# Cross-attention on one core: head groups of 3 and 2, keys stored once, and earlier refills

## The chip, the cores and the metric

The kernel runs on one core of a Trainium2 chip. The core has a matrix engine (PE), a vector engine (DVE), an activation engine (ACT), GpSimd (POOL) and a queue engine (SP) that issues most of the DMAs. Each engine works through its own list of instructions in order and waits for the others by semaphores. The metric is the time of one execution on the device in microseconds (us); lower is better.

## The reference, cut to what matters

Four attentions are computed in the original layer (text, object, others, IP), but the context given here has 77 tokens and the text part takes the first 77. The other three get no keys, so their sums are empty and add nothing. What remains is one cross-attention with a projection, a bias and a residual:

```python
q = heads(x @ to_q_w)              # x: 32 x 512 x 640, 20 heads of 32
k = heads(ctx @ to_k_w)            # ctx: 32 x 77 x 1024
v = heads(ctx @ to_v_w)
p = softmax(q @ k.T / sqrt(32))    # per head, 512 queries x 77 keys
out = merge(p @ v) @ to_out_w + to_out_b + x
```

All arrays are float32.

## The kernel before

Each float32 operand of a matmul is split into a high and a low part (`split`), and a product is made of three matmuls: high by high, high by low, low by high (`PAIRS`).

**The fill.** The context has 32 x 77 = 2464 tokens, cut into five groups of up to 512 columns (`GROUPS_KV`, the last is number `LAST`). For each, keys and values are projected for the five chunks j of 128 columns (four heads each). `split_keys` splits a chunk of keys in a tile `ks` (two buffers) and writes it to DRAM (`k_dram`), by five DMAs; those of the earlier groups are issued by POOL, those of the last by SP. `split_values` does the same for `v_dram`. The values of the last group are left over: their chunks are made by `context_values(LAST, j, psv)`, one before the first slot and four within slots 0, 1 and 2 (`beside`).

**The slots.** Then come 160 slots n, one for each batch b (0 to 31) and chunk j (0 to 4), written out by hand in `slot`. A slot holds four sets of scores (`scores(n, t)`, L478, 128 queries each): three matmuls of the query tile `qt` against the key tile `kb`, a maximum on DVE (`nm`, L486), four exponentials on ACT (L496). Between the sets PE makes the queries of the next slot (`queries`, L443), the values of slot n - 4 (`values`, L570) and eight of the forty steps of an earlier batch's output projection (`piece`, `project`, L613). DVE transposes the probabilities in blocks (`transpose_p`, L518, tile `z`); four DMAs write them to a DRAM tile `pd` (L525), and two more read them back transposed as `raw` (`load_p`, L534 and L535), two slots later. ACT, DVE and POOL split `raw` into `pp` (L542, L548, L549, L556) at the start of the slot that uses it, before that slot's exponentials.

**Keys and values by groups.** The five chunks are in two groups, j = 0, 1 and j = 2, 3, 4 (`GROUPS`). Each group has one tile of keys (`kb`) and one of values (`vb`), which are refilled in place for the next batch, so a refill must follow the last reader and precede the first. `refill(b, j, part)` says in which slot what is loaded, half of it at the start of the slot (part 0) and half in its middle (part 1): values of group 1 in slot j = 0, keys of group 1 in slot 1, values of group 0 in slot 2, keys of group 0 of the next batch in slot 3. Scores use the keys in the slot of their own j; values are used four slots later.

The key tile has four planes: two hold the high parts twice, since the first score matmul reads planes 0 and 3 (`kb[:, 0::3]`) and the others read planes 1 and 2, in which high and low parts of the two pairs of heads lie in opposite halves of the partitions. `k_dram` has three planes, laid out so that one DMA a head fills three planes of `kb`.

**The order of the rest.** SP issues nearly everything: the `pd` writes, `raw`, keys, values, the batch's x (`load_x`, in four quarters of the columns, `xs`), the residual rows (`xr`, L602, three buffers) and the results (L648). Tables in the code fix the slot of each: `TRANSPOSE_X` (DVE transposes of x, in three places of a slot), `SPLIT_X`, `RESIDUAL`, `BIAS` (POOL adds the bias to the residual), `PIECES`, `WO` (the output weights, first used in batch 1).

Of the kernel before, what the change touches and what calls it, by code (L numbers as in the profile page):

```python
# [8 lines left out]
F32 = mybir.dt.float32  # L9
FPR = mybir.dt.float32r  # L10
# [13 lines left out]
P = 128  # L24
Q = 32
HEADS = 20
HD = 32
NKEY = 77
HPC = 4
# [14 lines left out]
    (1, 1, 96, 2, 0, 32),  # L44
]

GROUPS = ((0, 2), (2, 3))
GROUP_OF = (0, 0, 1, 1, 1)


@with_exitstack
def kernel(
# [25 lines left out]
    nc = tc.nc  # L78
    B, S, C = x.shape
    CA = ehs.shape[2]  # L80
    NT = B * NKEY
# [12 lines left out]

    k_dram = [dram.tile([P, 3, nj, NT], FPR, name=f"k_dram{j0}") for j0, nj in GROUPS]

    v_dram = dram.tile([NT + KPAD - NKEY, HPC, NC_, 3, HD], FPR, name="v_dram")
    wo_dram = dram.tile([P, NC_, 2, C], FPR, name="wo_dram")  # L100
# [106 lines left out]
    def split_keys(g, j):  # L207
        g0, gn = GROUPS_KV[g]
        ks = kvt.tile([P, 2, G], FPR, tag="ks", name="ks")
        split(ks[:, 0, :gn], ks[:, 1, :gn], pks.pop(j)[:, :gn])  # L210
        engine = nc.gpsimd if g + 1 < len(GROUPS_KV) else nc.sync
        j0 = GROUPS[GROUP_OF[j]][0]
        dst = k_dram[GROUP_OF[j]].rearrange("(h r) s c n -> r s h c n", h=2)[
            :, :, :, j - j0, g0 : g0 + gn
        ]
        engine.dma_start(dst[:, 0].bitcast(F32), ks[:64, :, :gn].bitcast(F32))
        engine.dma_start(dst[:, 1, 0].bitcast(F32), ks[:64, 0, :gn].bitcast(F32))
        engine.dma_start(dst[:, 1, 1].bitcast(F32), ks[64:, 0, :gn].bitcast(F32))
        for half in range(2):
            engine.dma_start(dst[:, 2, half].bitcast(F32), ks[64:, 1 - half, :gn].bitcast(F32))  # L220

    def values_of(g, j, pool):

# [21 lines left out]
    def context_values(g, j, pool):  # L245
        values_of(g, j, pool)
        split_values(g, j)
# [3 lines left out]
    def load_x(b, quarters=range(4)):  # L251

        if b not in xss:
            xss[b] = xpool[0].tile([P, S // Q, C // 4], F32, tag="xs", name="xs")
        xs = xss[b]
        src = x[b].rearrange("(a j) (q u) -> q j a u", j=Q, q=4)
        for q in quarters:
            nc.sync.dma_start(xs[q * Q : (q + 1) * Q, :, :], src[q])
# [158 lines left out]
    def load_keys(b, g, heads=range(HPC)):  # L417
        j0, nj = GROUPS[g]
        src = k_dram[g][:, :, :, b * NKEY : (b + 1) * NKEY].bitcast(F32)
        for i in heads:  # L420
            r, half = slice(i * HD, (i + 1) * HD), i % 2 * NKEY
            nc.sync.dma_start(  # L422
                kbs[g][r, i // 2 : i // 2 + 3, :, half : half + NKEY].bitcast(F32), src[r]
            )

    def load_values(b, g, segments=SEGMENTS):
        j0, nj = GROUPS[g]
# [63 lines left out]
    def exps(n, t, sc, nm):  # L491
        if t == 0:
            sms[n] = main.tile([P, NQ * HPC], F32, tag="sm", name="sm", bufs=2)
        for i in range(HPC):
            at = t * HPC + i
            nc.scalar.activation(  # L496
                pnb[n % 2][:, at, :NKEY],
                sc[:, i * NKEY : (i + 1) * NKEY],
                AF.Exp,
                bias=nm[:, i : i + 1],  # L500
                accum_out=sms[n][:, at : at + 1],
            )
# [102 lines left out]
    def add_bias(b, t):  # L605
        nc.gpsimd.tensor_tensor(xrs[b, t], xrs[b, t], bias, ALU.add)  # L606
# [48 lines left out]


    PIECES = {3: (1, 0), 4: (1, 2), 0: (2, 4), 1: (2, 6), 2: (2, 8)}
    RESIDUAL = {2: (1, 0), 3: (1, 1), 4: (1, 2), 0: (2, 3)}
    BIAS = {3: (1, 0), 4: (1, 1), 0: (2, 2), 1: (2, 3)}
    TRANSPOSE_X = {0: ((), (0,), ()), 1: ((1,), (2,), ()), 2: ((3,), (), ())}  # L660
    SPLIT_X = {2: ((0,), (1,)), 3: ((2, 3), (4,))}

    WO = {4: (0,), 5: (1, 2), 6: (3, 4)}
    wos = []

    def take(m):
# [5 lines left out]
    def refill(b, j, part):  # L672

        heads = range(2 * part, 2 * part + 2)
        segments = SEGMENTS[4 * part : 4 * part + 4]
        if j == 0 and b:
            load_values(b - 1, 1, segments)
        elif j == 1:
            load_keys(b, 1, heads)
        elif j == 2:  # L680
            load_values(b, 0, segments)
        elif j == 3 and b + 1 < B:
            load_keys(b + 1, 0, heads)

    def slot(n, beside=()):
        b, j = divmod(n, NC_)
        ahead, more = n + 1 < N, b + 1 < B
        back, first = PIECES[j]
        bo_, has_out = b - back, b >= back
        xsplits = SPLIT_X.get(j, ((), ())) if more and n > 2 else ((), ())  # L690
        turns = TRANSPOSE_X.get(j, ((), (), ())) if more and b else ((), (), ())
        if b == 1 and j < 2:
            turns = (((), (), ()), ((0, 1), (2,), ()))[j]
        taken = takes.get(n)

        filling = taken is not None and not has_out
        if not filling:
            refill(b, j, 0)
        if taken is not None:
            cast_p(taken)  # L700
        if n - 1 in takes:
            high_a(takes[n - 1])
        bias_now = j in BIAS and b >= BIAS[j][0]
        if bias_now and (j == 3 or not ahead):
            add_bias(b - BIAS[j][0], BIAS[j][1])
        s = scores(n, 0)
        if j == 2:
            finish()
        if taken is not None:
            rest_p(taken)  # L710
        rs = sums(n - 1) if n else None
        if taken is not None:
            last_p(taken)
        if n:
            normalize(n - 1, rs)
        if n - 1 in takes:
            low_a(takes[n - 1])
        exps(n, 0, *s)
        if ahead:
            queries(n + 1, 0, 2)  # L720
        s = scores(n, 1)
        if n >= LATE:
            load_p(n - LAG + 1)
        if filling:
            refill(b, j, 0)
        if n == NC_:
            load_x(b + 1, (2, 3))
        for k in WO.get(n, ()):
            nc.sync.dma_start(wos[0][:, k].bitcast(F32), wo_dram[:, k].bitcast(F32))
        refill(b, j, 1)  # L730
        finish()
        if j == 4 and b and b + 2 < B:
            load_x(b + 2, (0, 1))
        if j in RESIDUAL and b >= RESIDUAL[j][0]:
            load_residual(b - RESIDUAL[j][0], RESIDUAL[j][1])
        exps(n, 1, *s)
        for i in turns[0]:
            transpose_x(b + 1, i)
        if ahead:
            queries(n + 1, 2, NC_)  # L740
        s = scores(n, 2)
        if not ahead:
            exps(n, 2, *s)
            piece(bo_, first)
            finish()
            s = scores(n, 3)
        early = ahead and has_out and j in (1, 4)
        if early:
            piece(bo_, first)
            finish()  # L750
        if not ahead:
            transpose_p(n - 1)
        if ahead:
            split_q(n + 1)
            if bias_now and j != 3:
                add_bias(b - BIAS[j][0], BIAS[j][1])
            exps(n, 2, *s)
        if n and not has_out:
            transpose_p(n - 1)
        if j == 4 and b + 2 < B:  # L760
            load_x(b + 2, (0, 1) if not b else (2, 3))
        for c in xsplits[0]:
            split_x(b + 1, c)
        if not ahead:
            exps(n, 3, *s)
            normalize(n, sums(n))
            finish()
            piece(bo_, first + 1)
            values(taken)
            sum_a(taken)  # L770
            return
        if has_out:
            if not early:
                piece(bo_, first)
        else:
            s = scores(n, 3)
        if taken is not None:
            values(taken)
        if len(beside) > 0:
            context_values(LAST, beside[0], psv)  # L780
        if has_out:
            s = scores(n, 3)
            transpose_p(n - 1)
        finish()
        for i in turns[1]:
            transpose_x(b + 1, i)
        if taken is not None:
            sum_a(taken)
        for c in xsplits[1]:
            split_x(b + 1, c)  # L790
        exps(n, 3, *s)
        if len(beside) > 1:
            context_values(LAST, beside[1], psv)
        if has_out:
            piece(bo_, first + 1)
        for i in turns[2]:
            transpose_x(b + 1, i)
# [86 lines left out]
        close(3)  # L884

    load_keys(0, 0)
    queries(0, 0, NC_)
    split_q(0)
    context_values(LAST, 0, psv)
# [1 line left out]
        transpose_x(1, i)  # L891
    for c in range(2):
        split_x(1, c)
    slot(0, (1,))
    slot(1, (2,))
    slot(2, (3, 4))
    kva.release()
    lw = ctx.enter_context(tc.tile_pool(name="lw", bufs=1, reuse_waits="tile"))
    wos.append(lw.tile([P, NC_, 2, C], FPR, name="wo_s"))
    psv.release()  # L900
    kvp.release()
    late.append(ctx.enter_context(tc.tile_pool(name="late", bufs=1, reuse_waits="tile")))
# [46 lines left out]
```

## Time and profile before

| what | us |
|---|---|
| median of 3 runs | 2124.54 |
| lowest and highest run | 2122.19, 2130.13 |
| profiled execution | 2130.74 |
| its span, first to last instruction | 2129.0 |
| PE busy in it | 1941.3 (91%) |
| weight loads of PE | 1716.1 (81%) |
| DVE busy | 1581.1 (74%) |
| ACT busy | 1552.7 (73%) |
| POOL busy | 1268.1 (60%) |
| first score matmul | 302.8 |

The span is what the profile explains; the profiled execution's own time is 1.7 us longer. The DMA queue that the hardware serves was busy for 79.5% of the span of its 16 engines, and the granted clock of PE was 0.953 of full speed on the mean. Busy shares are means over the fill and the slots, which have different limits, so a stretch has to be looked at by itself.

### The profile page before, as it was taken

What the parts mean: (1) busy time and instruction counts of PE and PEld (TensorE: products, weight loads), DVE (VectorE), ACT (ScalarE), POOL (GpSimd) and SP (SyncE); (2) the same over time, 40 slices, a digit from 0 to 9 for tenths busy, and PEclk for the clock granted to TensorE, in tenths of its full rate; (3) what the DMA queues carried; (4) which work ended last, traced back from release to release, by engine and by line L of the source; (5) the groups of instructions that cost most, each with busy time, mean ns of one, the idle gap of its engine ahead of it and who ended that gap; (6) DMA issues with size and microseconds to landing.
All of it is one profiled execution on the core that took longest, in us unless ns stands there. A gap on an engine that the chain in (4) does not pass through costs nothing.

```text
span 2129.0 us, 37333 instructions
## 1 busy us (share of the span) xinstructions
PE 1941.3 (91%) x10332; PEld 1716.1 (81%) x10332; DVE 1581.1 (74%) x2494; ACT 1552.7 (73%) x6210; POOL 1268.1 (60%) x1068
## 2 busy tenths in 40 slices
PE   9898978799999999999999999999999999999998
PEld 7776867688888888888888888888888888888887
DVE  4344336688788788887888888888878888888784
ACT  3232137788788788888888888888878888888782
POOL 1212246566666666666666666666767766666663
PEclk9999989899999999999999999999999999999999
DMA  9978868888788888888888888888888888888875
GB/s 183 207 188 230 202 142 195 216 215 215 203 214 219 205 218 213 213 216 212 221 223 214 208 220 218 217 218 208 223 207 217 211 216 209 215 216 212 210 202 150
DMA packets 584926, 443.96 MB, mean 209 GB/s; under 512 B 209104, under 2 KB 491792, under 8 KB 584720
## 3 DMA queue, kind: packets, MB, share of 16 engines
q1 hardware_dynamic: 577648, 421.83, 79.5%
q0 software_dynamic: 6976, 19.59, 3.3%
q8 instruction: 85, 1.39, 0.3%
q14 instruction: 121, 0.99, 0.1%
q10 hardware_dynamic: 96, 0.16, 0.0%
HBM read 253.48 MB, written 187.95 MB: 207 GB/s over the span
## 4 chain that ended last, share of the span: by engine, by line
PE 56%; DMA 17%; DVE 8%; SPq 8%; ACT 6%; issue 3%; POOL 1%; DVEq 0%; ACTq 0%; POOLq 0%
PE pq L443 21%; PE po L613 16%; PE sc L478 8%; PE pa L570 6%; DMA kb<-k_dram 5%; PE pk L191 5%; DMA raw<-pd 4%; SPq L422 2%; ACT pn L496 2%; DMA pd<-z 2%; DMA xs<-in_x_dram 2%; DMA k_dram<-ks 2%; DVE z L518 2%; SPq L525 2%; PE pv L191 1%
## 5 line engine op out<-in xcount | busy, mean ns | idle before, releaser
L496 ACT ACTIVATE pn<-sc,nm 128x77 f32<-128x77 f32 x2560 | 801.3, 332 | 123.5 <-DVE nm L486 114.0
L443 PE MATMUL pq<-xt,wq_s 128*128 128x512 f32 x2400 | 665.5, 421 | 0.1
L613 PE MATMUL po<-wo_s,at 128*128 128x320 f32 x3840 | 639.1, 315 | 9.8 <-DVE xr L642 4.0
L613 PEld LDWEIGHTS po<-wo_s,at 128*128 128x128 f32 x3840 | 570.5, 190 | 19.1 <-DVE at L595 10.8
L496 ACT ACTIVATION_READ_ACCUMULATOR pn<-sc,nm 128x1 f32 x2560 | 538.8, 210 | 0.0
L443 PEld LDWEIGHTS pq<-xt,wq_s 128*128 128x128 f32 x2400 | 459.5, 203 | 85.0 <-POOL xt L270 0.5
L478 PEld LDWEIGHTS sc<-kb,qt 128*128 128x128 f32 x1920 | 339.8, 197 | 201.1 <-issue 112.7
L556 POOL TENSOR_TENSOR pp<-raw,pp 64x512 fp32r<-64x512 f32 x160 | 225.1, 1407 | 439.7 <-ACT pp L548 362.9
L478 PE MATMUL sc<-kb,qt 128*128 128x154 f32 (+1 forms) x1920 | 330.8, 282 | 146.4 <-DMA kb<-k_dram 99.0
L486 DVE TENSOR_REDUCE nm<-sc 128x4 f32<-128x308 f32 x640 | 295.1, 466 | 163.1 <-PE sc L478 152.4
L511 POOL TENSOR_TENSOR pn<-pn,rs 128x1232 f32<-128x1232 f32 x160 | 364.4, 2277 | 49.1 <-DVE rs L506 38.5
L460 DVE TENSOR_TENSOR qt<-pq,qt 64x512 fp32r<-64x512 f32 x320 | 220.2, 688 | 110.2 <-ACT qt L454 105.1
L570 PE MATMUL pa<-pp,vb 128*128 128x512 f32 x960 | 253.3, 399 | 5.6 <-DMA vb<-v_dram 4.1
L518 DVE STREAM_TRANSPOSE z<-pn 128x1280 f32<-128x1280 f32 x160 | 241.8, 1512 | 21.0 <-DMA pd<-z 13.9
L270 POOL TENSOR_TENSOR xt<-xs,xt 128x512 fp32r<-128x512 f32 x160 | 203.8, 1292 | 86.3 <-ACT xt L269 60.3
L583 DVE TENSOR_TENSOR pa<-pa,aw 64x512 f32<-64x512 f32 x320 | 222.7, 696 | 28.0 <-ACT aw L581 17.7
L549 DVE TENSOR_TENSOR pp<-raw,pp 128x1024 fp32r<-128x1024 f32 x160 | 212.1, 1325 | 28.5 <-ACT pp L542 28.5
L542 ACT CAST pp<-raw 128x1024 fp32r<-128x1024 f32 x160 | 168.6, 1054 | 84.2 <-DMA raw<-pd 84.1
L458 POOL CAST qt<-qt 64x512 fp32r<-64x512 f32 x320 | 195.4, 610 | 48.7 <-ACT qt L454 30.9
L606 POOL TENSOR_TENSOR xr<-xr,bias 128x640 f32<-128x640 f32 x128 | 200.4, 1567 | 12.9 <-PE sc L478 2.9
L581 ACT COPY aw<-pa 64x1024 f32<-64x1024 f32 x160 | 162.0, 1013 | 59.7 <-PE pa L570 56.2
L570 PEld LDWEIGHTS pa<-pp,vb 128*128 128x128 f32 x960 | 174.6, 189 | 36.8 <-DMA vb<-v_dram 4.6
(47 smaller groups left out, 1550.6 us busy)
## 6 DMA issues: line engine op xcount, KB each, us to landing
pd<-z SPq DMA_DIRECT2D x640, 160.0 KB, 3.3
raw<-pd SPq DMA_DIRECT2D x160, 512.0 KB, 4.4
xs<-in_x_dram SPq DMA_DIRECT2D x128, 320.0 KB, 8.1
xr<-in_x_dram SPq DMA_DIRECT2D x128, 320.0 KB, 3.8
out_dram<-xr SPq DMA_DIRECT2D x127, 320.0 KB, 3.7
raw<-pd SPq DMA_DIRECT2D x160, 128.0 KB, 4.6
v_dram<-vs SPq DMA_DIRECT2D x80, 192.0 KB, 4.0
kb<-k_dram SPq DMA_DIRECT2D x128, 86.6 KB, 4.9
```

Of the source, the lines that this page charges most:

```text
L443: nc.tensor.matmul(pqs[n], wq_s[:, k, a, j * P : (j + 1) * P], xts[b, k][:, c, :], start=(k == 0 and m == 0), stop=(k == NC_ - 1 and m == 2),)
L460: nc.vector.tensor_tensor(qt[r, 1 + w, :], pq[r], qt[r, 0, :].bitcast(F32), ALU.subtract)
L478: nc.tensor.matmul(sc[:, cols], qt[:, m, t * P : (t + 1) * P], keys_, start=(m == 0), stop=(m == 2),)
L486: nc.vector.tensor_reduce(nm, sc[:, :KCOLS].rearrange("p (h k) -> p h k", k=NKEY), AX.X, ALU.max, negate=True)
L496: nc.scalar.activation(pnb[n % 2][:, at, :NKEY], sc[:, i * NKEY : (i + 1) * NKEY], AF.Exp, bias=nm[:, i : i + 1], accum_out=sms[n][:, at : ...
L511: nc.gpsimd.tensor_tensor(pf, pf, rs.unsqueeze(2).to_broadcast([P, NQ * HPC, NKEY]), ALU.mult)
L518: nc.vector.transpose(z.rearrange("p b t j -> p t b j"), pn.rearrange("p (t h) k -> p t (h k)", t=NQ).rearrange("p t (b i) -> p t b i", i=Q),)
L549: nc.vector.tensor_tensor(pp[:, 2:4, :], raw[:, 0:2, :], pp[:, 0:2, :].bitcast(F32), ALU.subtract)
L556: nc.gpsimd.tensor_tensor(pp[64:, 4, :], raw[:64, 2, :], pp[:64, 4, :].bitcast(F32), ALU.subtract)
L570: nc.tensor.matmul(pas[n][:, p, :], vb[:, p, t, :], pp[:, c, :], start=(c == p), stop=(t == 1),)
L583: nc.vector.tensor_tensor(pa[64 * p : 64 * p + 64, 0], pa[:64, p], aw[:, p], ALU.add)
L613: nc.tensor.matmul(pos[b, t, h][:, :HALF], ats[b * NC_ + j][:, a, t * P : (t + 1) * P], wos[0][:, j, c, h * HALF : (h + 1) * HALF], start= ...
```

## The change

Head groups become j = 0, 1, 2 and j = 3, 4. `k_dram` has two planes, high and low, as `ks` has them, and is written by one DMA. A head's keys are loaded by two DMAs, one for each part, into planes 1 and 2 of `kb`; the second copies of the high parts (planes 0 and 3) are made by two GpSimd copies, in slot 1 for group 1 and in slot 4 for group 0.

The refills move: keys of group 1 to slot 0, values of group 1 to slot 1; values of group 0 stay in slot 2 and keys of group 0 in slot 3. The last quarter of x is loaded at the start of slot 0 instead of the end of the slot 4 before it, and the transposes of x move later. The first residual and its bias are handled one slot earlier. The output weights are loaded a chunk a slot from slot 1 on. Two chunks of the last group's values are made before slot 0, and one beside each of the slots 0, 1 and 2; the tile of the output weights is allocated after slot 0.

```diff
-GROUPS = ((0, 2), (2, 3))
-GROUP_OF = (0, 0, 1, 1, 1)
+GROUPS = ((0, 3), (3, 2))
+GROUP_OF = (0, 0, 0, 1, 1)
...
-    k_dram = [dram.tile([P, 3, nj, NT], FPR, name=f"k_dram{j0}") for j0, nj in GROUPS]
+    k_dram = [dram.tile([P, 2, nj, NT], FPR, name=f"k_dram{j0}") for j0, nj in GROUPS]
...
-        dst = k_dram[GROUP_OF[j]].rearrange("(h r) s c n -> r s h c n", h=2)[
-            :, :, :, j - j0, g0 : g0 + gn
-        ]
-        engine.dma_start(dst[:, 0].bitcast(F32), ks[:64, :, :gn].bitcast(F32))
-        engine.dma_start(dst[:, 1, 0].bitcast(F32), ks[:64, 0, :gn].bitcast(F32))
-        engine.dma_start(dst[:, 1, 1].bitcast(F32), ks[64:, 0, :gn].bitcast(F32))
-        for half in range(2):
-            engine.dma_start(dst[:, 2, half].bitcast(F32), ks[64:, 1 - half, :gn].bitcast(F32))
+        engine.dma_start(
+            k_dram[GROUP_OF[j]][:, :, j - j0, g0 : g0 + gn].bitcast(F32), ks[:, :, :gn].bitcast(F32)
+        )
...
         for i in heads:
-            r, half = slice(i * HD, (i + 1) * HD), i % 2 * NKEY
-            nc.sync.dma_start(
-                kbs[g][r, i // 2 : i // 2 + 3, :, half : half + NKEY].bitcast(F32), src[r]
-            )
+            own, half = slice(i * HD, (i + 1) * HD), slice(i % 2 * NKEY, (i % 2 + 1) * NKEY)
+            other = slice(*((i + 2) % HPC * HD + k for k in (0, HD)))
+            for part, rows in enumerate((own, other)):
+                nc.sync.dma_start(kb[rows, 1 + i // 2, :, half], src[own, part])
+
+    def copy_keys(g):
+        kb = kbs[g]
+        nc.gpsimd.tensor_copy(kb[:64, 0], kb[:64, 1].bitcast(F32))
+        nc.gpsimd.tensor_copy(kb[64:, 3], kb[64:, 2].bitcast(F32))
...
-    RESIDUAL = {2: (1, 0), 3: (1, 1), 4: (1, 2), 0: (2, 3)}
-    BIAS = {3: (1, 0), 4: (1, 1), 0: (2, 2), 1: (2, 3)}
-    TRANSPOSE_X = {0: ((), (0,), ()), 1: ((1,), (2,), ()), 2: ((3,), (), ())}
+    RESIDUAL = {1: (1, 0), 3: (1, 1), 4: (1, 2), 0: (2, 3)}
+    BIAS = {2: (1, 0), 4: (1, 1), 0: (2, 2), 1: (2, 3)}
+    TRANSPOSE_X = {0: ((), (), (0,)), 1: ((), (1,), (2,)), 2: ((3,), (), ())}
...
-    WO = {4: (0,), 5: (1, 2), 6: (3, 4)}
+    WO = {1: (0,), 2: (1,), 3: (2,), 4: (3,), 5: (4,)}
...
-        if j == 0 and b:
+        if j == 0:
+            if not part and b and b + 1 < B:
+                load_x(b + 1, (3,))
+            load_keys(b, 1, heads)
+        elif j == 1 and b:
             load_values(b - 1, 1, segments)
-        elif j == 1:
-            load_keys(b, 1, heads)
...
-        if n == NC_:
-            load_x(b + 1, (2, 3))
...
-        if j == 4 and b and b + 2 < B:
+        if j == 4 and b + 2 < B:
             load_x(b + 2, (0, 1))
...
+            if j == 1:
+                copy_keys(1)
+            elif j == 4:
+                copy_keys(0)
             exps(n, 2, *s)
...
         if j == 4 and b + 2 < B:
-            load_x(b + 2, (0, 1) if not b else (2, 3))
+            load_x(b + 2, (2,))
...
     load_keys(0, 0)
+    copy_keys(0)
...
-    slot(0, (1,))
-    slot(1, (2,))
-    slot(2, (3, 4))
+    context_values(LAST, 1, psv)
+    slot(0, (2,))
     kva.release()
     lw = ctx.enter_context(tc.tile_pool(name="lw", bufs=1, reuse_waits="tile"))
     wos.append(lw.tile([P, NC_, 2, C], FPR, name="wo_s"))
+    slot(1, (3,))
+    slot(2, (4,))
```

More of the change, by code (lines that the diff above doesn't have):

```diff
@@ L419, in load_keys @@
         src = k_dram[g][:, :, :, b * NKEY : (b + 1) * NKEY].bitcast(F32)
+        kb = kbs[g].bitcast(F32)
         for i in heads:
-            r, half = slice(i * HD, (i + 1) * HD), i % 2 * NKEY
-            nc.sync.dma_start(
-                kbs[g][r, i // 2 : i // 2 + 3, :, half : half + NKEY].bitcast(F32), src[r]
-            )
+            own, half = slice(i * HD, (i + 1) * HD), slice(i % 2 * NKEY, (i % 2 + 1) * NKEY)
[6 more added lines that the diff above has]
+        nc.gpsimd.tensor_copy(kb[64:, 3], kb[64:, 2].bitcast(F32))
     def load_values(b, g, segments=SEGMENTS):
@@ L691, in slot @@
         turns = TRANSPOSE_X.get(j, ((), (), ())) if more and b else ((), (), ())
-        if b == 1 and j < 2:
-            turns = (((), (), ()), ((0, 1), (2,), ()))[j]
         taken = takes.get(n)
@@ L703, in slot @@
         bias_now = j in BIAS and b >= BIAS[j][0]
-        if bias_now and (j == 3 or not ahead):
+        if bias_now and not ahead:
             add_bias(b - BIAS[j][0], BIAS[j][1])
@@ L754, in slot @@
             split_q(n + 1)
-            if bias_now and j != 3:
+            if bias_now:
                 add_bias(b - BIAS[j][0], BIAS[j][1])
+            if j == 1:
+                copy_keys(1)
+            elif j == 4:
+                copy_keys(0)
             exps(n, 2, *s)
```

## The prediction

> **What bounds the kernel now.** I read the page's chain of waits first. PE holds 56% of it, and one transfer, the keys from DRAM, is the largest share that is not work. In the groups kept apart by shape, the first score matmul of a set owns most of PE's idle time.
>
> ```profile
> PE 56%; DMA 17%; DVE 8%; SPq 8%; ACT 6%; issue 3%; POOL 1%; DVEq 0%; ACTq 0%; POOLq 0%
> PE pq L443 21%; PE po L613 16%; PE sc L478 8%; PE pa L570 6%; DMA kb<-k_dram 5%; PE pk L191 5%; DMA raw<-pd 4%; SPq L422 2%; ACT pn L496 2%; DMA pd<-z 2%; DMA xs<-in_x_dram 2%; DMA k_dram<-ks 2%; DVE z L518 2%; SPq L525 2%; PE pv L191 1%
> ```
>
> ```profile
> L478 PE MATMUL sc<-kb,qt 128*128 128x308 f32 x640 | 205.6, 321 | 141.4 <-DMA kb<-k_dram 99.0 <-ACT pp L542 29.8 <-DMA pd<-z 9.5
> ```
>
> Then PE's timeline over one batch in mid-run (start, duration, instructions). Four score sets make a slot, five slots (j = 0 to 4) a batch. Shown: the end of slot j=1 and the start of j=2.
>
> ```profile
> 1206.13 0.49 PE L478 MATMUL sc<-kb,qt 128*128 128x308 f32 x3
> 1206.45 1.58 PE L443 MATMUL pq<-xt,wq_s 128*128 128x512 f32 x6
> ...
> 1214.18 1.96 PE L613 MATMUL po<-wo_s,at 128*128 128x320 f32 x12
> 1219.39 0.72 PE L478 MATMUL sc<-kb,qt 128*128 128x308 f32 x3 [3.25 <-DMA kb<-k_dram]
> 1219.94 2.16 PE L443 MATMUL pq<-xt,wq_s 128*128 128x512 f32 x6
> 1221.90 0.80 PE L478 MATMUL sc<-kb,qt 128*128 128x308 f32 x3
> 1222.50 3.05 PE L443 MATMUL pq<-xt,wq_s 128*128 128x512 f32 x9
> ```
>
> PE stands 3.25 us, then runs slowly: nine pq take 3.05 us where the other slots have 2.29. SP's timeline tells why the keys are late: the first two of four loads go out at 1210.75, the last two at 1213.52, behind a reload of `raw`, for use at 1216.
>
> ```profile
> 1210.75 1.50 SPq L422 DMA_DIRECT2D kb<-k_dram  x2
> 1212.34 0.60 SPq L534 DMA_DIRECT2D raw<-pd  x1
> 1212.99 0.47 SPq L535 DMA_DIRECT2D raw<-pd  x1
> 1213.52 1.24 SPq L422 DMA_DIRECT2D kb<-k_dram  x2
> ```
>
> Last, busy time by stage (columns: length; PE, PEld, DVE, ACT, POOL busy; clock; DMA share; GB/s): batches 2 to 30, then slots j=0, 1, 2, 3, 4 of that batch.
>
> ```profile
> 418.40:2025.70 1607.30, 1495.28 (x8267) 1337.17 (x8266) 1321.13 (x2089) 1339.55 (x5512) 1075.05 (x842) 0.96 0.85 215
> 1196.33:1206.13 9.80, 9.80 (x59) 8.89 (x58) 7.84 (x14) 8.86 (x40) 6.86 (x6) 1.00 1.06 266
> 1206.13:1219.39 13.26, 10.01 (x60) 8.85 (x58) 12.67 (x20) 10.14 (x42) 6.65 (x6) 1.00 0.91 237
> 1219.39:1231.06 11.67, 11.67 (x58) 10.34 (x59) 7.49 (x13) 8.16 (x34) 7.43 (x6) 0.85 0.63 180
> 1231.06:1240.89 9.83, 9.83 (x59) 8.93 (x59) 8.50 (x15) 9.22 (x38) 8.59 (x7) 1.00 0.76 198
> 1240.89:1250.99 10.10, 10.10 (x59) 8.94 (x59) 8.48 (x15) 9.85 (x44) 8.37 (x8) 1.00 0.95 213
> ```
>
> Slots 0, 3 and 4 are PE without a gap. Slot 1 carries the idle time, slot 2 the slow clock (0.85). A mean batch is 1607.3/29 = 55.42 us.
>
> **The key wait, steady batches.** Keys of the second group are loaded in slot 1 and read from slot 2; afterwards they are loaded in slot 0 and read from slot 3, and the first group in slot 3 for the next slot 0. The longest key landing in the trace is 7.6 us after issue; the lead becomes some 20 us. So the wait goes entirely. Without it slot 1 is its 10.0 us of PE work (10.01 busy), and slot 2, at full clock, the same order of matmuls: 10.0. Batch: 9.83 + 10.0 + 10.0 + 9.84 + 10.1 = 49.8 us. That is 5.6 less; 29 batches give 164 us, the last batch (its own wait 2.1) 2 more.
>
> **What becomes late next.** At 49.8 us a batch, by the shares of 1321.13, 1339.55 and 1075.05 us, DVE needs 45.6, ACT 46.2, POOL 37.1: each fits, ACT with 3.6 us to spare. But ACT loses some of it: it waited 84.1 us in 58 pieces for `raw` (about 2.6 us a batch; in this batch 1.39 us at the start of slot 1 and 0.91 at slot 2). Slot 2's gap has let ACT, DVE and POOL catch up each time; that cushion goes. At slot 1 ACT runs some 4 us behind PE, and the value matmuls (L570) find their POOL operand ready 0.2 us before they start: slots 1, 2 and 4 have next to no slack. So part of the `raw` lateness reaches PE. From below 0; from above all 2.6 us. Slots 3 and 4, in which ACT is fullest (9.22 and 9.85 us), show PE unbroken, so I sit near the lower end: 0.6 us a batch, 17 us in all.
>
> **SP's queue.** Key issues go from 8 to 16 a batch. An old one takes 0.62 to 0.75 us above (192 or 288 pieces). A new one has 64 or 96, like a value load of 32 rows; the four value loads in the middle of a slot took 2.01 and 2.03 us, so 0.5 each: 8.0 for 5.5 us. SP's timeline sums to 40.4 us of issuing in this batch; 43 of 50.4 is full but fits. Slot 0 gains one issue, slot 1 five, slot 3 four; slots 2 and 4 lose one each. In slot 0 the last quarter of x and half the keys now stand before `raw`'s reload in place of half the values, and in slot 1 half the values in place of half the keys; `raw` delayed is ACT delayed, which is in the 0.6. The key writes into slots 0 and 3 wait for readers that finished before the preceding `pd` write was issued: no new wait. The residual moved to slot 1 waits for a store issued a slot-half earlier (3.7 us to landing): about nothing; without that cover, up to 1 us on SP.
>
> The Trainium skill, page "DMA: Bandwidth & Descriptors", section "Rules for kernel authors", speaks against this: coalesce, since under 64 KB a DMA is mostly overhead; the new key loads are 20 and 30 KB where the old were 58 and 87. Its section "Anatomy of one DMA" gives about 2.0 us fixed; in series 8 more a batch would be an estimated 16 us, and the result over 2500 us. The rows here show otherwise: value loads of 24 KB land 2.9 us after issue and are issued four in 2.0 us, so the fixed part overlaps.
>
> **DMA engines.** A third of the key packets goes: 20 fewer 32-partition rows, 640 of 308 bytes a batch. At the page's mean of 79.5% x 16 x 2129 us / 577,648 = 47 ns that is 1.9 us of all engines, by bytes (308 of 730 on average) 0.8. Against 0.85 x 55.42 = 47.1 now, some 46 remain: 92% of 50. Not counted as a gain; it is the second rival's subject. Moving one quarter of x (320 KB) from slot 4 to 0 takes load from 0.95 to a slot already at 1.06, but behind the same bytes as before.
>
> **GpSimd's copies.** Four a batch, 64x462 and 64x308, beside casts of 64x512 that take 610 ns: about 0.55 and 0.37 us, 1.8 us a batch. They stand after the bias addition, in the idle time in which POOL waits for ACT (L556, 362.9 us in all, 11 a batch). Without that cover they cost 1.8 x 29 = 52 us. The bias moved from slot 3 to 2 is the same work on the same engine. The DVE transposes moved later in slots 0 and 1 are as many as before.
>
> **The start.** Before the first score (302.8 us) PE idles 15.4 us for the keys and 7.8 and 3.3 us at 201 and 136 us. In the chain there, `ks` splits wait for two buffers: POOL issues five DMAs (0.60 + 4 x 0.52 = 2.7 us) and the last lands 3.4 us later. With one DMA 2.1 us go from each of two such rounds a group; the last group saves four SP issues of 0.6 in the round that matters and in the key reload behind it. Three groups at 3 to 4 us, and about 5 for the last: 15. The first copy adds 1.1 us ahead of the first scores. Pulling one chunk of values (4.6 us of PE) into the wait gives 4.6 back in the slots. Output weights over slots 1 to 5 instead of 4 to 6: batch 1 takes 64.6 us with one stall of 9.5 us behind transfers; 0 to 9. Sum 5 to 32; I take 22, as the chain has other members (values, x) close by.
>
> **Sum.** 164 + 2 - 17 + 22 = 171 us. The profiled execution took 2130.74 us (span 2129.0 and 1.7 around it); that is 6.2 above the median of 2124.54. I subtract from the median: **1954 us** (1960 for an execution like the profiled one).
>
> **Rivals.**
> 1. *DMA takes over.* The transfers keep the share of time they have in this stage (0.85 to 0.86): 46/0.86 = 53.5 us a batch, a gain of 1.9 x 29 + 2 + 22 = 80: 2045. For: the queue is over-full in slot 0, and `raw` is already late. Against: slots 4 and 0 ran at 0.95 and 1.06 with PE unbroken.
> 2. *SP becomes the bound, slower.* If a key issue costs 0.7 us whatever its size, SP issues 40.4 + 5.6 = 46.0 us a batch. Its waits for the transposed tile (L525 on DVE, 363.8 us, 11.4 a batch) follow in order; if none of them shrink, a batch is 57.4, +2.0 x 29 - 22 = +36: 2160. It decides once issues and unshrinkable waits pass 55.4 us. Against: value loads of that size, and those waits are mostly SP being early.
> 3. *The keys stay late* (the load is held in SP's order, or POOL's copy is): only the start's gain, 2102. Against: two slots of lead.
>
> **How the numbers follow.** Forecast 0.70, own range 1922 (no stalls, 32 from the start) to 1990; rival 1 0.18; rival 2 0.07; rival 3 0.03; 0.02 for something near no change. The range for 8 in 10 runs from 1922 into rival 1: 2030, which is about 2.3 us of stall a batch. 0.5% (some 10 us) is about what can be told from no change here; by that, faster 0.91, same 0.02, slower 0.07.
>
> **What would show it.** Right: no PE idle time on kb in slots 2 and 3, the clock at 1.00 through a whole batch, slots of 9.8 to 10.5 us, first score near 285. Wrong: PE idle before L570 or scores on ACT, POOL or vb of over 2 us a batch (rival 1: `raw` waits grow), SP never idle (rival 2), or a clock that still drops each batch.

## The result, and the profile after

The changed kernel takes 2062.33 us (median of 4 runs, 2058.71 to 2063.8) against 2127.01 us before; the ratio is 0.9695, 95% interval 0.967 to 0.972. It is faster, by some 65 us, where 171 were forecast, and 2062 lies above the range that was given (1922 to 2030).

The two profiled executions, 2129.0 and 2062.0 us of span, can be cut at the same two places, the first score matmul of slot 10 and of slot 155:

| stretch | before | after | gained | forecast |
|---|---|---|---|---|
| to slot 10 (start, batches 0 and 1) | 418.4 | 375.9 | 42.5 | 22 |
| batches 2 to 30 | 1607.3 | 1582.7 | 24.6 | 147 |
| the rest | 103.2 | 103.4 | -0.2 | 2 |

So the start gave twice what was forecast, and the steady batches a sixth. A batch went from 55.42 to 54.58 us, not to 50.4.

The wait for keys is gone as forecast: the scores waited 99.0 us for the key transfers before and wait 0.3 us now. In the groups by shape, the first score matmul of a set waits for something else, and the cast of `raw` on ACT, 84.1 us of waiting before, hardly waits:

```profile
PE sc L479 <- DMA kb<-k_dram: 0.3, 1, 0.3
```

```profile
L479 PE MATMUL sc<-kb,qt 128*128 128x308 f32 x640 | 202.1, 316 | 58.5 <-POOL kb L425 48.7 <-DMA xs<-in_x_dram 4.9 <-ACT pn L497 3.7
L543 ACT CAST pp<-raw 128x1024 fp32r<-128x1024 f32 x160 | 168.9, 1056 | 1.8 <-DMA raw<-pd 1.8
```

L425 is the second of GpSimd's two key copies. The chain of waits, by engine, has turned over. PE had 56% of it; now DVE has the most:

```profile
DVE 35%; PE 17%; issue 14%; ACT 12%; DMA 9%; POOL 6%; SPq 6%; DVEq 0%; POOLq 0%; ACTq 0%
```

Busy time by stage (length; PE, PEld, DVE, ACT, POOL busy; clock; DMA share; GB/s): batches 2 to 30, then the slots j = 0 to 4 of one batch and slot 0 of the next.

```profile
375.90:1958.60 1582.70, 1497.54 (x8266) 1313.70 (x8266) 1313.48 (x2089) 1338.25 (x5510) 1206.95 (x957) 0.99 0.83 214
1140.10:1150.20 10.10, 10.10 (x58) 9.14 (x59) 6.64 (x12) 7.44 (x34) 7.18 (x5) 1.00 0.92 277
1150.20:1160.08 9.88, 9.88 (x60) 8.95 (x59) 8.62 (x16) 8.11 (x34) 6.08 (x5) 1.00 0.75 194
1160.08:1170.34 10.26, 10.12 (x59) 8.93 (x59) 9.36 (x16) 7.85 (x37) 7.58 (x7) 1.00 0.83 216
1170.34:1180.57 10.23, 10.11 (x59) 8.97 (x59) 8.97 (x15) 9.73 (x41) 9.29 (x8) 1.00 0.69 156
1180.57:1194.00 13.43, 10.77 (x59) 8.78 (x58) 11.64 (x18) 12.99 (x50) 11.48 (x11) 1.00 1.03 229
1194.00:1205.80 11.80, 11.79 (x57) 10.40 (x58) 6.73 (x12) 7.55 (x34) 7.39 (x5) 0.86 0.87 243
```

Slots 1 and 2, 13.9 and 11.8 us on the mean before, are 9.9 and 10.3 now. But slot 4 went from 10.1 to 13.4, and slot 0 from 9.8 to 10.1 or, in 12 of the 29 batches, 11.7 to 11.8 at a lower clock. PE's timeline at the end of slot 4 shows two waits:

```profile
1185.66 0.49 PE L614 MATMUL po<-wo_s,at 128*128 128x320 f32 x2
1187.07 0.85 PE L614 MATMUL po<-wo_s,at 128*128 128x320 f32 x4 [0.92 <-DVE at L596]
1187.76 1.56 PE L571 MATMUL pa<-pp,vb 128*128 128x512 f32 x6
1189.16 0.49 PE L479 MATMUL sc<-kb,qt 128*128 128x308 f32 x3
1189.48 2.85 PE L614 MATMUL po<-wo_s,at 128*128 128x320 f32 x18
1193.99 0.97 PE L479 MATMUL sc<-kb,qt 128*128 128x308 f32 x3 [1.66 <-POOL kb L425]
1194.76 2.85 PE L444 MATMUL pq<-xt,wq_s 128*128 128x512 f32 x6
```

And POOL's timeline shows what the copies stand behind:

```profile
1180.94 3.78 POOL L265 TENSOR_TENSOR xt<-xs,xt 128x512 fp32r<-128x512 f32 x3
1186.18 1.27 POOL L557 TENSOR_TENSOR pp<-raw,pp 64x512 fp32r<-64x512 f32 x1 [1.46 <-issue]
1187.52 2.28 POOL L512 TENSOR_TENSOR pn<-pn,rs 128x1232 f32<-128x1232 f32 x1
1189.86 1.28 POOL L459 CAST qt<-qt 64x512 fp32r<-64x512 f32 x2
1191.22 1.56 POOL L607 TENSOR_TENSOR xr<-xr,bias 128x640 f32<-128x640 f32 x1
1192.74 0.56 POOL L424 CAST kb<-kb 64x462 fp32r<-64x462 f32 x1
1193.36 0.57 POOL L425 CAST kb<-kb 64x462 fp32r<-64x462 f32 x1
1195.42 2.33 POOL L557 TENSOR_TENSOR pp<-raw,pp 64x512 fp32r<-64x512 f32 x1 [1.49 <-ACT pp L549]
```

From 1186.18 on POOL is busy without a break until the copies end at 1193.93, and PE's scores start 0.06 us later. The two idle pieces of POOL, 1.46 us before the first work that belongs to slot 4 and 1.49 us after the copies, are both there, but on the wrong sides of it. What makes POOL start at 1186 is read from the chain of waits in order of time (start, duration): ACT, with the three x splits (xt) of slot 3, reaches the cast for slot 4 late.

```profile
1178.80 1.37 ACT pn L497 x8
1180.17 1.04 ACT xt L264 x2
1181.22 1.01 ACT aw L582
1182.24 0.52 ACT xt L264
1183.01 1.11 ACT pn L497 x7
1184.12 0.61 ACT pp L543
...
1186.18 1.28 POOL pp L557
```

### The profile page after: what moved, and what is told of

It reads as the page before. It is cut to its first block, busy times and chain, and to the rows that moved or that the text cites. A ratio compares the mean times of both kernels' runs of the same rounds, so it can differ in the third digit from the quotient of the medians.

```text
span 2062.0 us, 37523 instructions
## 1 busy us (share of the span) xinstructions
PE 1938.3 (94%) x10332; PEld 1690.2 (82%) x10332; DVE 1571.7 (76%) x2494; ACT 1551.5 (75%) x6210; POOL 1368.4 (66%) x1116
## 4 chain that ended last, share of the span: by engine, by line
DVE 35%; PE 17%; issue 14%; ACT 12%; DMA 9%; POOL 6%; SPq 6%; DVEq 0%; POOLq 0%; ACTq 0%
DVE z L519 8%; ACT pn L497 7%; DVE nm L487 5%; PE pq L444 5%; DVE pp L550 5%; DVE qt L461 5%; DMA raw<-pd 4%; DVE pa L584 3%; DVE xs L257 3%; PE po L614 3%; DMA xs<-in_x_dram 3%; PE sc L479 2%; DVE at L596 2%; PE pk L191 2%; PE pv L191 2%
## 5 line engine op out<-in xcount | busy, mean ns | idle before, releaser
L614 PE MATMUL po<-wo_s,at 128*128 128x320 f32 x3840 | 641.0, 315 | 35.2 <-DVE at L596 28.4
L444 PE MATMUL pq<-xt,wq_s 128*128 128x512 f32 x2400 | 647.6, 410 | 3.5 <-POOL xt L265 0.3
L614 PEld LDWEIGHTS po<-wo_s,at 128*128 128x128 f32 x3840 | 571.8, 190 | 46.1 <-DVE at L596 37.1
L557 POOL TENSOR_TENSOR pp<-raw,pp 64x512 fp32r<-64x512 f32 x160 | 304.6, 1904 | 369.3 <-ACT pp L549 301.2
L444 PEld LDWEIGHTS pq<-xt,wq_s 128*128 128x128 f32 x2400 | 438.5, 195 | 93.5 <-POOL xt L265 16.6
L479 PE MATMUL sc<-kb,qt 128*128 128x154 f32 (+1 forms) x1920 | 342.1, 281 | 66.4 <-POOL kb L425 48.7
L571 PE MATMUL pa<-pp,vb 128*128 128x512 f32 x960 | 256.5, 402 | 5.2 <-DVE at L596 2.4
L550 DVE TENSOR_TENSOR pp<-raw,pp 128x1024 fp32r<-128x1024 f32 x160 | 202.5, 1266 | 29.7 <-ACT pp L543 29.7
L571 PEld LDWEIGHTS pa<-pp,vb 128*128 128x128 f32 x960 | 173.8, 189 | 43.3 <-DVE at L596 11.9
```

Source lines behind the costliest of these rows:

```text
L444: nc.tensor.matmul(pqs[n], wq_s[:, k, a, j * P : (j + 1) * P], xts[b, k][:, c, :], start=(k == 0 and m == 0), stop=(k == NC_ - 1 and m == 2),)
L479: nc.tensor.matmul(sc[:, cols], qt[:, m, t * P : (t + 1) * P], keys_, start=(m == 0), stop=(m == 2),)
L550: nc.vector.tensor_tensor(pp[:, 2:4, :], raw[:, 0:2, :], pp[:, 0:2, :].bitcast(F32), ALU.subtract)
L557: nc.gpsimd.tensor_tensor(pp[64:, 4, :], raw[:64, 2, :], pp[:64, 4, :].bitcast(F32), ALU.subtract)
L571: nc.tensor.matmul(pas[n][:, p, :], vb[:, p, t, :], pp[:, c, :], start=(c == p), stop=(t == 1),)
L614: nc.tensor.matmul(pos[b, t, h][:, :HALF], ats[b * NC_ + j][:, a, t * P : (t + 1) * P], wos[0][:, j, c, h * HALF : (h + 1) * HALF], start= ...
```

## The experiments

Each kernel is named by its label. The batch given is the mean of batches 2 to 30 in the profiled execution; after the change it is 54.58 us. Times are medians of 4 runs, ratios are to the kernel before, run beside each of them.

### copy_first: the copies where POOL idles

```diff
+        if j == 4:
+            copy_keys(0)
         if taken is not None:
             last_p(taken)
...
             if j == 1:
                 copy_keys(1)
-            elif j == 4:
-                copy_keys(0)
```

> The changed kernel with the key copies of group 0 moved, in slot 4, ahead of last_p on GpSimd, into its idle 1.5 us there. Theory A (the scores of slot 0 stand behind POOL's queue: last_p, normalize, casts, bias, copies; the cushion is there otherwise): the 1.6 us of PE idle time on kb L425 go, with them most of the half clock in every other slot 0 (0.7 us a batch) : a batch of about 52.0 instead of 54.6, in all 1975 to 2000. Rival B (the lost cushion: a chain of DVE and ACT sets the batch whatever the copies do): less than 0.8 us a batch, 2040 to 2062, and PE idle at another operand.

Measured: 1980.71 us, ratio 0.9309 (0.9279 to 0.9338); batch 51.83. Theory A holds. POOL's and PE's timelines of one slot 4:

```profile
1145.57 0.56 POOL L424 CAST kb<-kb 64x462 fp32r<-64x462 f32 x1
1146.19 1.46 POOL L425 CAST kb<-kb 64x462 fp32r<-64x462 f32 x1
1147.72 1.28 POOL L557 TENSOR_TENSOR pp<-raw,pp 64x512 fp32r<-64x512 f32 x1
1149.08 2.28 POOL L512 TENSOR_TENSOR pn<-pn,rs 128x1232 f32<-128x1232 f32 x1
1151.42 1.28 POOL L459 CAST qt<-qt 64x512 fp32r<-64x512 f32 x2
```

```profile
1147.98 0.86 PE L614 MATMUL po<-wo_s,at 128*128 128x320 f32 x4 [0.91 <-DVE at L596]
...
1150.41 2.85 PE L614 MATMUL po<-wo_s,at 128*128 128x320 f32 x18
1153.09 0.49 PE L479 MATMUL sc<-kb,qt 128*128 128x308 f32 x3
```

The scores follow the projection without a gap. The second copy takes 1.46 us here, longer than in its old place, and the batch is still 2.75 us shorter: place decided, not work. The clock stays at 1.00 through the 29 batches, so the slow slots 0 went with the idle time:

```profile
375.70:1878.90 1503.20, 1465.97 (x8268) 1296.59 (x8267) 1308.77 (x2089) 1331.94 (x5513) 1207.82 (x958) 1.00 0.86 226
```

### no_copy: no copies at all

```diff
-            if j == 1:
-                copy_keys(1)
-            elif j == 4:
-                copy_keys(0)
...
     load_keys(0, 0)
-    copy_keys(0)
```

> The changed kernel without the key copies at all; planes 0 and 3 of the key tiles stay zero, so the high-by-high products are left out of the scores. Theory A: their place cost the time, not their 1.8 us of GpSimd work: within 10 us of copy_first, 1970 to 1995. Rival C (the copies slow DVE through a shared path, or fill POOL): 20 us or more below copy_first. Rival B: 2040 to 2062 as well.

Measured: 1978.98 us, ratio 0.9304 (0.9271 to 0.9337); batch 51.83, the same as copy_first to the hundredth, with 83 us less of POOL's work over the 29 batches (1124.70 against 1207.82). The copies as work cost nothing; rival C falls.

```profile
371.10:1874.20 1503.10, 1466.16 (x8267) 1296.54 (x8267) 1308.59 (x2089) 1331.41 (x5512) 1124.70 (x842) 1.00 0.86 226
```

### three_planes: the moved refills without the new key scheme

The three-plane `k_dram`, its five writes and the one load a head are those of before; groups and refills are those of the change.

```diff
-    k_dram = [dram.tile([P, 2, nj, NT], FPR, name=f"k_dram{j0}") for j0, nj in GROUPS]
+    k_dram = [dram.tile([P, 3, nj, NT], FPR, name=f"k_dram{j0}") for j0, nj in GROUPS]
...
-            for part, rows in enumerate((own, other)):
-                nc.sync.dma_start(kb[rows, 1 + i // 2, :, half], src[own, part])
+            nc.sync.dma_start(
+                kbs[g][r, i // 2 : i // 2 + 3, :, half : half + NKEY].bitcast(F32), src[r]
+            )
...
```

> The changed kernel with keys stored three times and loaded by one DMA a head as before the change, so without copies; groups of 3 and 2 and all moved refills kept. Theory A: steady batches as in no_copy (about 52), the start some 10 us later since the five writes of each key chunk are back: 1980 to 2010. Rival D (DMA or SP bound: a third more key packets, 8 issues fewer): packets matter, raw waits grow again, batches of 53.5 or more, 2025 or above.

Measured: 2012.91 us, ratio 0.9462 (0.9433 to 0.9491); batch 51.87. The steady part is as expected under theory A: 640 packets more and 8 issues fewer a batch, taken together, change nothing that shows. The total is 3 us above the expected range, because the start came out later than the 10 us allowed: first score at 303.8 us, against 274.9 in copy_first.

### old_fill: the order of the start as before

```diff
-    WO = {1: (0,), 2: (1,), 3: (2,), 4: (3,), 5: (4,)}
+    WO = {4: (0,), 5: (1, 2), 6: (3, 4)}
...
-    context_values(LAST, 1, psv)
-    slot(0, (2,))
+    slot(0, (1,))
+    slot(1, (2,))
+    slot(2, (3, 4))
```

> The changed kernel with the order of the start as before the change: one chunk of values ahead of slot 0, four in slots 0 to 2, output weights in slots 4 to 6. The start gave 42.5 us (slot 10 begins at 375.9 instead of 418.4). Theory E (the single key write of the fill gives about 25, the order the rest): 2075 to 2085, the first score near 273 plus nothing, slots 0 to 9 longer. Rival F (the order gives nearly all): 2090 to 2105. Steady batches unchanged at 54.6.

Measured: 2068.05 us, ratio 0.9729 (0.9691 to 0.9766); batch 54.54; slot 10 at 381.8 us against 375.9. The order is worth some 6 us at slot 10, less than theory E allowed it. That is small but there: the change and the five kernels here that keep its start and leave no work out (copy_first, turns_early, turns_spread, high_first, spread_high) put slot 10 at 374.2 to 377.9 us. In the total the intervals of the two kernels overlap (0.967 to 0.972 for the change). Most of the start's gain must lie elsewhere.

### five_writes: the key write of the start in five pieces

On copy_first; the bytes and planes stay.

```diff
-        engine.dma_start(
-            k_dram[GROUP_OF[j]][:, :, j - j0, g0 : g0 + gn].bitcast(F32), ks[:, :, :gn].bitcast(F32)
-        )
+        dst = k_dram[GROUP_OF[j]][:, :, j - j0, g0 : g0 + gn].bitcast(F32)
+        for r0, r1 in ((0, 32), (32, 64), (64, 96), (96, 112), (112, P)):
+            engine.dma_start(dst[r0:r1], ks[r0:r1, :, :gn].bitcast(F32))
```

> copy_first with each write of a key chunk in the start cut into five DMAs by rows, the same bytes. With three_planes the first score came at 303.8, here at 274.9. If the number of issues on POOL and SP makes the difference: first score at 292 or later, in all 1996 to 2012. If the third plane's bytes do: within 6 us of copy_first, 1980 to 1987.

Measured: 1999.58 us, ratio 0.942 (0.9386 to 0.9454); batch 51.84. The first score in the three forms, from PE's timelines of the change, of five_writes and of three_planes (the bracket is PE's idle time before it):

```profile
272.89 0.41 PE L479 MATMUL sc<-kb,qt 128*128 128x308 f32 x1 [0.94 <-POOL kb L425]
```

```profile
290.68 1.17 PE L479 MATMUL sc<-kb,qt 128*128 128x308 f32 x2 [11.23 <-POOL kb L425]
```

```profile
303.81 0.94 PE L478 MATMUL sc<-kb,qt 128*128 128x308 f32 x3 [11.88 <-DMA kb<-k_dram]
```

Against copy_first, slot 10 is 18.2 us later with five issues, and another 13.7 us later with the third plane too. The first is what five issues in place of one cost for the same bytes; the second also holds the other key loads and the missing first copy, so the third plane's bytes alone are not measured. The total lies in the range of the first expectation, the first score just short of its 292 us; but five issues give only a part of the 32 us between copy_first and three_planes.

### no_x_load: a tenth of the DMA traffic away

```diff
     def load_x(b, quarters=range(4)):
+        if b > 1:
+            xss[b] = xss[1]
+            return
```

> copy_first with the loads of x (1.3 MB a batch of some 13) left out from batch 2 on; transposes and splits work on what lies in the tile. Rival I (DMA load and late raw): the raw waits go and a batch falls to 50.5 or less, 1935 to 1950. Theory G and rival H: 51.3 or more, 1965 to 1981.

Measured: 1980.74 us, ratio 0.9329 (0.9289 to 0.9369); batch 51.84. ACT's casts of `raw`, in copy_first and here, and the stage:

```profile
L543 ACT CAST pp<-raw 128x1024 fp32r<-128x1024 f32 x160 | 168.7, 1055 | 22.4 <-DMA raw<-pd 20.4 <-POOL kb L425 0.9 <-POOL kb L424 0.4
```

```profile
L546 ACT CAST pp<-raw 128x1024 fp32r<-128x1024 f32 x160 | 169.1, 1057 | 1.5 <-DMA raw<-pd 1.0 <-POOL kb L427 0.4
```

```profile
376.20:1879.60 1503.40, 1465.38 (x8266) 1295.68 (x8266) 1308.60 (x2089) 1331.34 (x5512) 1210.88 (x958) 1.00 0.76 200
```

The DMA share falls from 0.86 to 0.76 and the waits for `raw` from 20.4 to 1.0 us, and the time stays where it was. Late `raw` and DMA load are not what is left (rival I).

### no_turns and no_split: DVE's transposes, ACT's and POOL's splits

Each on copy_first, from batch 2 on; first no_turns, then no_split.

```diff
     def transpose_x(b, i):
+        if b > 1:
+            return
```

> copy_first with the DVE transposes of x (four of 0.82 us a batch, slots 0 to 2) left out from batch 2 on. Theory G: 51.4 or more a batch, 1965 to 1981. Rival H (DVE has no idle time in slots 1 and 2, its lag is handed to ACT's splits): 50.3 or less, 1935 to 1945.

Measured: 1932.77 us, ratio 0.9104 (0.9072 to 0.9137); batch 50.15.

```profile
376.80:1831.30 1454.50, 1438.80 (x8268) 1295.18 (x8267) 1225.63 (x1973) 1328.54 (x5513) 1159.14 (x958) 1.00 0.89 233
```

```diff
     def split_x(b, c, high=nc.scalar.copy, low=nc.gpsimd):
+        if b > 1:
+            xts[b, c] = xts[1, c]
+            return
```

> copy_first with the splits of x (ACT high part, GpSimd low part) left out from batch 2 on; all later batches use batch 1's. A batch of copy_first is 51.8 us where PE's work is 49.8. Theory G (the remaining 2.0 us come from the five splits that ACT and POOL do in slots 2 and 3, 3.2 and 6.5 us a batch): 49.8 to 50.3 a batch, in all 1922 to 1940. Rival H (DVE's unbroken chain) or I (late raw, DMA): at most 0.7 us a batch, 1960 to 1981.

Measured: 1950.98 us, ratio 0.9192 (0.9159 to 0.9226); batch 50.97. This one has a wait that copy_first has not: its early copies stand on POOL for the key loads of slot 3, 38.7 us in 30 pieces.

```profile
POOL kb L428 <- DMA kb<-k_dram: 38.7, 30, 2.1
```

Of the 2.0 us that copy_first's batch has over PE's 49.8, 1.7 go without the transposes and 0.9 without the splits. They add up to more than there is, so they are not two separate costs. The chain of waits of copy_first, in order of time, shows links of one chain in slots 3 and 4: DVE, then ACT with exponentials and x splits, then DVE's split of the attention output, which PE waits for.

```profile
1131.73 1.51 DVE z L519
...
1137.07 0.54 DVE at L596
...
1139.71 1.37 ACT pn L497 x8
1141.08 1.03 ACT xt L264 x2
...
1145.02 0.94 ACT pp L543
...
1145.99 0.81 DVE pp L550
...
1147.38 0.56 DVE at L596
...
1147.98 0.86 PE po L614 x4
```

Before 1130.5 us this chain runs back to the landing of a store, so that the transposes of slots 0 to 2 belong to it rests on no_turns alone. Rival H is right about the larger link. Theory G's number was too large, and no_split lies between the two ranges that were expected of it.

### turns_early, turns_spread, high_first, spread_high: moving the links

All on copy_first.

```diff
 # turns_early; turns_spread has {0: ((), (0,), (1,)), 1: ((), (2,), (3,))}
-    TRANSPOSE_X = {0: ((), (), (0,)), 1: ((), (1,), (2,)), 2: ((3,), (), ())}
+    TRANSPOSE_X = {0: ((), (0,), ()), 1: ((1,), (2,), ()), 2: ((3,), (), ())}
...
-            if not part and b and b + 1 < B:
-                load_x(b + 1, (3,))
...
-            load_x(b + 2, (2,))
+            load_x(b + 2, (2, 3))
```

> copy_first with x's last quarter loaded in slot 4 again and the DVE transposes of x back in their places before the change (slot 0 middle, slot 1 middle and end of the third set, slot 2). If the later places are what costs DVE its cushion: 0.5 to 1.2 us a batch less, 1945 to 1967. If only the number of transposes in slots 0 to 2 counts: 1975 to 1986.

> copy_first with x loaded in slot 4 and two transposes each in slots 0 and 1, none in slot 2, so that DVE enters slots 2 to 4 with less behind it. Theory H (DVE's lag after slot 2 is handed to ACT's and POOL's splits and reaches PE in slots 2 to 4): slots 2 to 4 shrink, 0.6 to 1.6 us a batch less, 1933 to 1963. If the lag only moves to slots 0 and 1: 1970 to 1990.

Measured: turns_early 1977.32 us, ratio 0.9302 (0.9265 to 0.9338), batch 51.65; turns_spread 2015.88 us, ratio 0.9481 (0.945 to 0.9512), batch 53.04. The places that the change gave the transposes cost nothing that can be told. Two in slot 1 behind two in slot 0 are worse by 35 us, outside both ranges expected: slot 2 grows from 10.3 to 11.1 us, and the value matmuls wait for the tile `pa` to be released by DVE, 24.9 us where copy_first has 0.7:

```profile
L571 PE MATMUL pa<-pp,vb 128*128 128x512 f32 x960 | 257.6, 403 | 30.0 <-DVE at L596 24.9 <-DMA vb<-v_dram 3.0 <-ACT pp L543 1.0
```

Theory H's remedy was wrong: DVE's lag is not worked off by moving its work forward.

```diff
 # high_first: in slot 4 alone
+        at_first = j == 4 and n - 1 in takes
+        if at_first:
+            high_a(takes[n - 1])
         if taken is not None:
             cast_p(taken)
...
+        if at_first:
+            low_a(takes[n - 1])
         if taken is not None:
             rest_p(taken)
...
```

> copy_first with, in slot 4 alone, the split of the attention output (L591 on ACT, L596 on DVE) ahead of the cast of raw and what follows it, since PE's first projection there waits 0.91 us for it. If that operand is the one late: the 0.91 us go and half of them or more is kept, 1950 to 1968. If all operands of slot 4 are late together: the wait moves to L571 (pp), 1974 to 1984.

> turns_spread and high_first together. If both act on the same lag, no better than the better of the two; if PE is then bound by its own work (49.8 us a batch): 1922 to 1940.

Measured: high_first 1975.1 us, ratio 0.9291 (0.9259 to 0.9323), batch 51.61; spread_high 2015.84 us, ratio 0.947 (0.943 to 0.9511), batch 53.11. In high_first the waits before L614 for DVE are gone (0.3 us in all, 28.5 in copy_first), and some of them come back before L571 (6.5 us for DVE's L596 and 5.4 for POOL, 0.7 and 0.2 in copy_first). Slot 4 falls from 11.64 to 11.18 us, and slot 2 grows from 10.27 to 10.48: half is given back. The interval overlaps with that of copy_first, so the gain is not established; the time lies in the second range that was expected. spread_high is no better than turns_spread.

## Why the prediction was wrong, point by point

**The step that failed** is the one on GpSimd's copies: "They stand after the bias addition, in the idle time in which POOL waits for ACT". The prediction's sum put their cost at nothing. The work was sized rightly (0.56 and 0.44 us measured for 0.55 and 0.37), and the idle time existed. But it lay where POOL's next operand was late, which here is behind the copies, while PE's next scores need them at once. What had to be asked is when POOL reaches the copies, against when PE reaches slot 0. The text named 52 us as the price without cover; measured by copy_first it is (54.58 - 51.83) x 29 = 80 us, more than the work itself, since the copies wait for all that POOL does before them (slot 4, 13.44 us on the mean against 11.64) and the clock then drops too (slot 0, 10.78 against 9.85).

**The lost cushion** had the right mechanism and was too small: 0.6 us a batch, taken near the lower end of 0 to 2.6. With the copies out of the way it is 51.83 - 49.8 = 2.0, 59 us in all. Its cause was also misplaced. The text put it on late `raw`; no_x_load removed those waits and gained nothing. The removals of DVE's transposes and of the x splits put it on the chain of DVE, ACT and POOL. The argument from slots 3 and 4 ("show PE unbroken") was weak, since those slots followed the stalls of slots 1 and 2, in which the other engines could catch up; that they did is argued, not tested by itself.

**The start** was undersized: 22 for 42.5. The forecast counted two buffer rounds a group and went no further along the chain; single writes against five are worth 18 us, the three-plane scheme with its five writes against copy_first 32 (407.6 to 375.7, the 18 among them), the order of the start some 6. The other 4 to 5 us were not taken apart. That the start gave 20 us more than forecast was luck for the total: it hid a part of the two errors above.

**Right:** the key wait went entirely. Of the 5.6 us a batch, copy_first has 3.6; no_turns reaches 5.3 (50.15 us), but with work left out. The 16 key issues, DMA load (rival 1) and SP (rival 2) do not bound it: three_planes and no_x_load leave the batch alone. The coalescing rule weighed in the prediction has a place in this kernel all the same: not at the key loads in the slots, but at the key writes of the start, where five issues instead of one stood on the chain. The 2.0 us that the prediction quotes beside it stand on that page under DMAs issued by GpSimd, and the key loads of the slots are issued by SP; with 8 or 16 of them a batch takes 51.87 or 51.83 us.

The sum, in measured terms: 164 for the waits, -59 for the cushion, -80 for the copies' place, +42.5 for the start, 0 at the end: 67, which is 2129.0 - 2062.0. It has to come out, since the terms of the batch are differences of three batch times. Against the forecast of 171, the copies took 80, the cushion 42 and the end 2 more, and the start gave 20 more. Two bounds of the prediction do not follow from its own terms: no stalls and 32 us from the start give 1926 us, not 1922, and 2030 us stands for 3.2 us of stall a batch with the start at 22, not for 2.3.

Left open: how much of the cushion is DVE's and how much ACT's and POOL's can't be told from two removals on one chain, and the five_writes kernel doesn't separate the third plane's bytes from the other key loads.

## What to carry to other kernels

Idle time of an engine covers new work only if it lies between the moment the new work can start and the moment its result is needed; read both from the timeline, at that place in the queue. When a regular stall is removed, look at what the other engines did during it: here DVE and ACT were busy for 82% and 83% of the steady batches, each stall left them time to catch up, and the slots measured just after it said little of how the kernel runs without. Where an engine's idle time comes right before a late operand, as POOL's 1.46 us here, that is the place for work that has its own operands already.

## What the hardware showed

In the change PE's clock dropped to half after 1.62 to 1.66 us of idle time, in 12 of the 29 batches and never in two in a row: slow stretches of 3.41 us begin at 976.1, 1085.3 and 1194.6 us, 109.2 us apart, which is two batches (53.9 and 55.5 us); elsewhere three batches lie between. In the 3.41 us before the last of these, PE stood for 1.66 us in one piece (1192.33 to 1193.99). Waits of 0.91 us never dropped the clock in batches 2 to 30 of copy_first. The Trainium skill, page "TensorE: Matmul & The Clock Gate", section "What's actually happening", has the clock fall after at least one idle window of some 3.4 us; here a stretch of that length that was idle for about half was enough in 12 batches, and waits of 1.63 to 1.66 us in the other 17 were not; what decides isn't shown.

GpSimd's copy of 64x462 took 0.57 us in the change and 1.38 us on the mean as the second copy in copy_first: the 30 that run beside DVE's two-input subtraction (L550) took 1.45 to 1.47 us, the other three 0.57. The skill's page "GPSIMD Engine Reference", section "8. Key points", names such contention; here it cost nothing, as the batch is that of no_copy (51.83 us).
